# An attention and ternary feed-forward block on one core: the last chunk gets an instruction order of its own

## The chip, the core and the metric

The kernel runs on one core of a Trainium2 chip. The core has five engines with a queue each, and every queue issues its instructions in the order in which the program names them: PE multiplies matrices, DVE and POOL compute elementwise, ACT evaluates functions, SP issues the transfers. Data lie in SBUF; PE writes its results to PSUM. The metric is the device time of one execution in microseconds (us), as the median of several runs. In the profile "PEld" is the loading of PE's weights, and L12 is line 12 of the kernel before.

## What is computed

The input has 8 sequences of 1024 rows of 512 numbers. It goes through causal attention with 16 heads of 32, with a score that falls by one per position, then through a feed-forward layer with quantized activations and ternary weights, each with a layernorm ahead of it, a layernorm behind it and a residual sum:

```python
scores = jnp.einsum('bhid,bhjd->bhij', Q, K) / jnp.sqrt(jnp.float32(hd))
scores = jnp.where(causal_mask, -jnp.inf, scores) + decay      # decay = -(i - j)
attn = jax.nn.softmax(scores, axis=-1)
...
xh = x @ H                                # Hadamard
xq = _quantize_activations(xh)            # 4 bits, scale = max|row| / 7
wq = _ternary_quantize_ste(weight)
return jnp.einsum('bsi,oi->bso', xq, wq)
...
x = x + _layernorm(_L0_attn_ref(_layernorm(x, axis=-1), ...), axis=-1)
x = x + _layernorm(_L0_ffn_ref(_layernorm(x, axis=-1), L0_ffn_weight), axis=-1)
```

## The kernel before, in words

The 8192 rows are cut into 16 chunks of 512 rows, a chunk into 4 tiles of 128 rows. Since the decay makes far keys negligible, a block of 128 queries looks only at its own keys and the 128 before. That this is allowed is shown by a bound on the scores, which is collected over the chunks in `allmax` and compared at the end of the chunk before the last (L832 to L834); the flag `ok` decides whether a general version runs behind the fast one.

**Attention.** A chunk has 8 units, one for each half of the chunk (256 queries) and each group of 4 heads. A unit goes through five steps. `scores` (L522) is 24 matmuls on PE and four exponentials on ACT, which write `pr`; the tile `s` in PSUM has one buffer, so the scores of a unit wait for the exponentials of the unit before. `mask` (L551, POOL) clears what lies ahead of the query. `add_keys` (L564, POOL) adds the two key blocks into `both`, which has one buffer. `values` (L574) is 24 matmuls with the values and 8 with ones over `both`, into `av`. `divide` (L602, four DVE instructions) writes the quotient into `oT`.

**Rest.** What follows for a tile is the generator `rest` (L167). Every `next` on it issues one step, up to a `yield`:

1. `xr`: the rows are loaded again (SP)
2. o: output projection, 8 matmuls
3. y: bias, statistics (DVE), then 1/sd and `ca` (POOL, L119, L120, L187)
4. `x1`, `u`, `w`: residual sum and the first two Hadamard stages, five DVE instructions (L190 to L199), each with two inputs in SBUF
5. wT: 4 transposes, copy (ACT)
6. h: 8 matmuls, Square with a sum on ACT (L219, its output `sq` is not used), 1/sd `rb` on POOL (L221, L222)
7. maximum `sc` of h (DVE, L229), its scaling by `rb` and the reciprocal `isc` (L230 to L233)
8. `qf` (ACT, L236), `qi` (DVE, L238)
9. qiT: 4 transposes, copy (ACT)
10. f: 4 matmuls
11. `y2` (DVE, L250)
12. statistics of `y2` (DVE), 1/sd and `cc` (POOL)
13. layernorm (ACT, L258), residual sum (POOL, L259), output (SP, L260)

**The order by hand.** Inside `manual_schedule` the order of calls is the order in every queue. In the loop over chunks (L736) each round handles two units (a "pair of slots") of a chunk, and between their steps it issues steps of two tiles, `rest_a` (the newer) and `rest_b` (the older, the `rest_a` of the round before), the projections of the next chunk (`proj`) and the norms of the one after. `next(rests_due)` hands out the next tile and lets the one after it issue its `xr`. A tile runs some six units behind the attention. `bank(...)` names which of three PSUM banks (`held`, `one`, `two`) the next product takes. The last chunk goes through the same loop with `proj` empty; its tiles 2 and 3 and the remaining steps of tile 1 follow in the tail (L836 to L840), in an order written as letters. Tile names here: 15.2 is tile 2 of chunk 15.

The buffers that matter: `y`, `u`, `w`, `wT`, `y2` one, `xr` and `pr` two, `x1` three.

Of the kernel before, what the change touches and what calls it, by code (L numbers as in the profile page):

```python
# [24 lines left out]
NG = H // HPG  # L25
# [9 lines left out]
SLACK = 1.01  # L35


BAND_LIMIT = 12.5
NORM, REST = 4, 13
@with_exitstack  # L40
def sandwich_kernel(
    ctx: ExitStack,
# [14 lines left out]
    nc = tc.nc  # L57
# [51 lines left out]
    allmax = const.tile([P, 1], F32, name="allmax")  # L109
# [57 lines left out]
    def rest(pools, n, row0, oT):  # L167
# [8 lines left out]
        row, small = pools.row, pools.small  # L176
# [15 lines left out]
        half = D // 2  # L192
        u = row.tile([P, D], F32, tag="u", name=f"u_{n}", bufs=1)
# [11 lines left out]
        wT = row.tile([P, KD, P], F32, tag="wT", name=f"wT_{n}", bufs=1)  # L205
        nc.scalar.copy(wT, pt)  # L206
        yield
        xh = pools.ps_m.tile([P, D], F32, tag="pm", name=f"h_{n}_ps")
        for k in range(KD):
# [4 lines left out]
                start=True,  # L214
                stop=True,
            )
        sq = row.tile([P, D], BF16, tag="xh2", name=f"xh2_{n}", bufs=1)
        var = small.tile([P, 1], F32, tag="var", name=f"var_{n}")
        nc.scalar.activation(sq, xh, AF.Square, accum_out=var)  # L219
        rb = small.tile([P, 1], F32, tag="rstd1", name=f"rstd_b_{n}")  # L220
        nc.gpsimd.tensor_scalar(rb, var, 1.0 / D, EPS, ALU.mult, ALU.add)  # L221
        nc.gpsimd.tensor_tensor(rb, rb, neghalf[:, :1], ALU.pow)  # L222
# [4 lines left out]

        sc = small.tile([P, 1], F32, tag="sc", name=f"sc_{n}")
        nc.vector.tensor_reduce(sc, xh, AX.X, ALU.max, apply_absolute_value=True)  # L229
        nc.vector.tensor_scalar(sc, sc, rb, SCALE_MIN, ALU.mult, ALU.max)  # L230
        isc = small.tile([P, 1], F32, tag="isc", name=f"isc_{n}")
        nc.vector.reciprocal(isc, sc)
# [13 lines left out]
        yield  # L246
        acc = project(pools, f"f_{n}", lambda k: qiT[:, k, :], lambda k: ternT[:, k, :])
        yield
        y2 = row.tile([P, D], F32, tag="y2", name=f"y2_{n}", bufs=1)
        nc.vector.scalar_tensor_tensor(y2, acc, sc, wscale_row, ALU.mult, ALU.mult)  # L250
        yield
        mvc = stats(small, y2, f"c_{n}")
# [25 lines left out]
    def band():  # L278
# [4 lines left out]
        big = es.enter_context(tc.tile_pool(name="big", bufs=2))  # L283
# [4 lines left out]
        small, row = pools.small, pools.row  # L288
# [199 lines left out]
        def diagonal(col, n):  # L488
            diag = row.tile([P, P], F32, tag="diag", name=f"diag_{n}", bufs=1)
            nc.vector.tensor_scalar(diag, ident, col, None, ALU.mult)  # L490
            return diag

        def spread_max(diag, n):

            ps = pools.ps_m.tile([P, P], F32, tag="pm", name=f"m_ps_{n}")
            nc.tensor.matmul(ps, ones, diag, start=True, stop=True)
            m = small.tile([P, 1], F32, tag="spread", name=f"spread_{n}")
            nc.vector.tensor_reduce(m, ps, AX.X, ALU.max)
            return m

        class Unit:
# [59 lines left out]
                    channel_multiplier=-1,  # L561
                )

            def add_keys(self):  # L564

                self.both = big.tile([P, HPG, 2, P], F32, tag="both", name=f"both_{self.n}", bufs=1)
                pr, r0 = self.pr, 1 if self.first else 0
                nc.gpsimd.tensor_tensor(  # L568
                    self.both[:, :, r0:], pr[:, :, r0:, 0, :], pr[:, :, r0:, 1, :], ALU.add
                )  # L570
                if self.first:
                    nc.gpsimd.tensor_copy(self.both[:, :, 0], pr[:, :, 0, 1, :])
# [44 lines left out]
        chunks = [Chunk(at) for at in range(B * NCHUNK)]  # L617
# [22 lines left out]
        ch = chunks[0]  # L640
# [6 lines left out]
        r = rstd_of(small, mv[:, :, 1], TPC, "rstd_x0")  # L647
# [13 lines left out]
        for i in range(3 * KD):  # L661
# [4 lines left out]
            which, o = divmod(i, KD)  # L666
# [32 lines left out]
        def steps(gen, count):  # L699
            for _ in range(count):  # L700
                if gen is not None:
                    next(gen)

        def products(proj, count):
            for _ in range(count):
                if proj:
                    proj.product()

        def drains(proj, count):
            for _ in range(count):  # L710
                if proj:
                    proj.drain()

        def ahead(gens):

            held = None
# [16 lines left out]
        held, one, two = 0, 1, 2  # L733
        unit = None
        rest_a = rest_b = None
        for at, ch in enumerate(chunks):  # L736
            before = chunks[at - 1] if ch.c else None
            nxt = chunks[at + 1] if at + 1 < len(chunks) else None
            proj = Projections(nxt, ch if nxt.c else None) if nxt else None
            ch.oT = [  # L740
                big.tile([P, NG, 2 * P], F32, tag="oT", name=f"oT_{ch.n}_{half}")
                for half in range(2)
            ]
            for u in range(0, 2 * NG, 2):

                new = Unit(ch, before, u)
                new.scores()
                if proj and u == 0:
                    proj.combine(0)
                if unit:  # L750
                    unit.values()
                    unit.divide()
                unit = new
                steps(rest_a, 1)
                if proj and u >= 4:
                    proj.square()
                unit.mask()
                unit.add_keys()
                bank(one)
                products(proj, 1)  # L760
                drains(proj, 1)
                norm = next(norms_due)
                steps(norm, 1)
                bank(two)
                products(proj, 1)
                drains(proj, 1)
                rest_b = rest_a
                bank(held)
                steps(rest_b, 1)
                steps(norm, 1)  # L770
                rest_a = next(rests_due) if at or u >= 4 else None
                bank(one)
                steps(rest_a, 1)
                bank(two)
                steps(rest_b, 1)
                steps(rest_a, 1)
                if proj and u == 0:
                    proj.combine(1)
                if proj and u >= 4:
# [11 lines left out]
                products(proj, 1)  # L791
                steps(rest_b, 1)
                if proj and u >= 4:
                    proj.largest()
                new.mask()
                steps(rest_a, 1)
                drains(proj, 1)
# [7 lines left out]
                products(proj, 1)  # L805
                drains(proj, 1)
                if u == 6:
                    bank(held)
                    steps(rest_a, 1)
                    bank(one)  # L810
                    products(proj, 1)
                    bank(two)
                    if proj:
                        proj.shift()
                    drains(proj, 1)
                    bank(held)
                    products(proj, 1)
                    drains(proj, 1)
                    bank(two)
                    held, two = two, held  # L820
                else:
                    bank(one)
                    steps(rest_a, 1)
                    bank(held)
                    products(proj, 1)
                    drains(proj, 1)
                    bank(one)
                    held, one, two = one, two, held
                steps(rest_a, 1)
                steps(rest_b, 1)  # L830
                steps(rest_a, 1)
            if at == len(chunks) - 2:  # L832
                okm = spread_max(diagonal(allmax, "all"), "all")
                nc.vector.tensor_scalar(ok, okm, (BAND_LIMIT / SLACK) ** 2, None, ALU.is_le)  # L834

        unit.values()  # L836
        unit.divide()
        tails = {"r": rest_a, "a": next(rests_due), "b": next(rests_due)}
        for which in "rrarbarrabraabaabbababaabbabbb":
            next(tails[which])  # L840
        es.close()


# [215 lines left out]
    ok = const.tile([P, 1], I32, name="ok")  # L1059
    with tc.manual_schedule():  # L1060
        band()
# [47 lines left out]
```

## Time and profile before

| what | us |
|---|---|
| median of 3 runs (lowest to highest) | 1482.47 (1480.69 to 1483.7) |
| the profiled execution | 1484.03 |
| its span, first to last instruction | 1482.3 |
| PE, DVE, POOL, ACT busy in it | 1385.1, 1020.1, 916.0, 686.7 |
| mean granted clock of PE | 0.981 |
| scores of the last chunk's first unit begin | 1354.11 |
| values of its last unit begin | 1430.97 |
| last instruction on POOL ends | 1478.12 |

The span is what the profile covers; the 1.7 us around it belong to the execution but to no instruction. Busy time of PE is the time in which matmuls were under way, which says little about how well they are used; the granted clock says what share of its full clock PE was given. In a timeline a line gives start and duration, engine, line, operation, output and inputs with their shapes, the count, and in brackets how long the engine had been idle and whom it waited for. In the chain of waits each line is a piece of the path that ended last.

### The profile page before, as it was taken

What the parts mean: (1) busy time and instruction counts of PE and PEld (TensorE: products, weight loads), DVE (VectorE), ACT (ScalarE), POOL (GpSimd) and SP (SyncE); (2) the same over time, 40 slices, a digit from 0 to 9 for tenths busy, and PEclk for the clock granted to TensorE, in tenths of its full rate; (3) what the DMA queues carried; (4) which work ended last, traced back from release to release, by engine and by line L of the source; (5) the groups of instructions that cost most, each with busy time, mean ns of one, the idle gap of its engine ahead of it and who ended that gap; (6) DMA issues with size and microseconds to landing.
All of it is one profiled execution on the core that took longest, in us unless ns stands there. A gap on an engine that the chain in (4) does not pass through costs nothing.

```text
span 1482.3 us, 29278 instructions
## 1 busy us (share of the span) xinstructions
PE 1385.1 (93%) x11508; PEld 970.8 (65%) x11508; DVE 1020.1 (69%) x2159; ACT 686.7 (46%) x1176; POOL 916.0 (62%) x1284
## 2 busy tenths in 40 slices
PE   5999999999999999999999999999999999997763
PEld 2476777767767776677767677666767777674431
DVE  1557767677777767777777777777777777675553
ACT  2344454545545454454545455454545545352431
POOL 2365757566575766667575666658666675663653
PEclk9999999999999999999999999999999999998995
DMA  4210110111011101101111111011101101000000
GB/s 152 70 31 14 44 44 31 35 44 44 23 44 44 43 24 44 44 29 37 44 43 32 35 44 35 31 44 44 34 32 44 44 23 37 29 30 15 29 29 23
DMA packets 31777, 57.87 MB, mean 39 GB/s; under 512 B 4240, under 2 KB 4368, under 8 KB 31632
## 3 DMA queue, kind: packets, MB, share of 16 engines
q1 hardware_dynamic: 30768, 54.87, 11.3%
q8 instruction: 93, 1.52, 0.5%
q10 hardware_dynamic: 864, 1.05, 0.2%
q14 instruction: 52, 0.43, 0.1%
HBM read 39.13 MB, written 16.78 MB: 38 GB/s over the span
## 4 chain that ended last, share of the span: by engine, by line
PE 72%; DVE 21%; POOL 3%; issue 2%; ACT 1%; DMA 1%; SPq 0%; POOLq 0%; ACTq 0%; DVEq 0%
PE o_ps L153 15%; PE k_ps L388 13%; PE q_ps L388 9%; PE v_ps L388 7%; PE s L530 7%; PE av L583 6%; PE h_ps L210 4%; PE av L592 3%; DVE u L195 2%; DVE w L198 2%; DVE w L199 2%; PE f_ps L153 2%; DVE x L190 2%; DVE st_a L126 2%; DVE y L183 2%
## 5 line engine op out<-in xcount | busy, mean ns | idle before, releaser
L543 ACT ACTIVATE pr<-s,bias 128x512 f32<-128x512 f32 (+1 forms) x512 | 295.9, 661 | 171.0 <-PE s L530 154.6
L568 POOL TENSOR_TENSOR both<-pr 128x1024 f32<-128x1024 f32 (+1 forms) x128 | 269.5, 2105 | 5.6
L153 PE MATMUL o_ps<-wo_sb,oT 128*128 128x512 f32 x512 | 239.8, 612 | 0.0
L554 POOL TENSOR_SCALAR_AFFINE_SELECT pr<-pr 128x1024 f32<-128x1024 f32 x128 | 152.4, 1191 | 124.3 <-ACT pr L543 124.1
L183 DVE TENSOR_TENSOR y<-o_ps,bo 128x512 f32<-128x512 f32 x64 | 44.3, 691 | 172.1 <-PE o_ps L153 172.1
L153 PEld LDWEIGHTS o_ps<-wo_sb,oT 128*128 128x128 f32 x512 | 94.7, 195 | 96.3 <-issue 95.4
L530 PE MATMUL s<-qT,kT 32*128 32x128 f32 (+1 forms) x2816 | 143.0, 330 | 0.0
L530 PEld LDWEIGHTS s<-qT,kT 32*128 32x128 f32 x2816 | 115.4, 187 | 32.9 <-issue 22.5
L583 PE MATMUL av<-pr,v 128*32 128x128 f32 (+1 forms) x2816 | 132.3, 318 | 0.0
L119 POOL TENSOR_SCALAR rstd_a<-mv_a 128x1 f32<-128x1 f32 x64 | 14.3, 224 | 181.4 <-DVE mv_a L127 181.4
L219 ACT ACTIVATE xh<-h_ps 128x512 bf16<-128x512 f32 x64 | 38.3, 598 | 155.7 <-PE h_ps L210 155.7
L141 ACT ACTIVATE xn<-xc,nmr,rstd_n 128x512 f32<-128x512 f32 x60 | 48.8, 813 | 127.0 <-POOL nmr L139 127.0
L583 PEld LDWEIGHTS av<-pr,v 128*32 128x32 f32 x2816 | 75.2, 110 | 38.2 <-issue 1.4
L229 DVE TENSOR_REDUCE sc<-h_ps 128x1 f32<-128x512 f32 x64 | 44.1, 690 | 69.8 <-ACT xh L219 69.8
L206 ACT COPY wT<-wT_ps 128x512 f32<-128x512 f32 x64 | 37.5, 586 | 116.7 <-PE wT_ps L204 116.7
L259 POOL TENSOR_TENSOR y<-y,x 128x512 f32<-128x512 f32 x64 | 81.7, 1276 | 1.9 <-ACT y L258 1.9
L592 PE MATMUL av<-both,ones 128*32 128x256 f32 x1024 | 79.3, 381 | 2.1 <-POOL both L568 2.1
L119 POOL TENSOR_SCALAR rstd_c<-mv_c 128x1 f32<-128x1 f32 x64 | 14.8, 231 | 98.4 <-DVE mv_c L127 97.6
L210 PE MATMUL h_ps<-had_sb,wT 128*128 128x128 f32 x512 | 69.0, 278 | 5.8 <-ACT wT L206 5.8
L210 PEld LDWEIGHTS h_ps<-had_sb,wT 128*128 128x128 f32 x512 | 67.5, 194 | 10.4 <-ACT wT L206 7.4
L153 PE MATMUL f_ps<-ternT,qiT 128*128 128x512 bf16 x256 | 67.4, 387 | 1.6 <-ACT qiT L245 1.6
L608 DVE STREAM_TRANSPOSE sumT<-av 128x256 f32<-128x256 f32 x128 | 55.4, 433 | 14.2 <-PE av L592 14.2
(194 smaller groups left out, 3051.1 us busy)
## 6 DMA issues: line engine op xcount, KB each, us to landing
xr<-in_x SPq DMA_DIRECT2D x64, 256.0 KB, 3.0
out<-y SPq DMA_DIRECT2D x64, 256.0 KB, 2.0
xc<-in_x SPq DMA_DIRECT2D x60, 256.0 KB, 2.9
wk_sb<-in_wkT ACTq DMA_DIRECT2D x4, 256.0 KB, 5.5
x<-in_x SPq DMA_DIRECT2D x4, 256.0 KB, 5.0
wq_sb<-in_wqT SPq DMA_DIRECT2D x4, 256.0 KB, 4.7
wf_sb<-in_wf SPq DMA_DIRECT2D x4, 256.0 KB, 5.4
wv_sb<-in_wvT SPq DMA_DIRECT2D x4, 256.0 KB, 5.2
```

What stands on the lines that cost most here:

```text
L153: nc.tensor.matmul(ps, lhs(k), rhs(k), start=(k == 0), stop=(k == KD - 1))
L183: nc.vector.tensor_tensor(y, ps, bo2, ALU.add)
L210: nc.tensor.matmul(xh[:, k * P : (k + 1) * P], wT[:, k, :], had_sb if k else had0_sb, start=True, stop=True,)
L259: nc.gpsimd.tensor_tensor(y2, y2, x1, ALU.add)
L388: nc.tensor.matmul(ps[:, o, :], a[:, i, osl], b[:, i, :], start=(i == 0), stop=(i == HB - 1))
L530: nc.tensor.matmul(s[:, hh, sc : sc + w], kc.kT[hsl, g, at * P : (at + 1) * P], ch.qT[hsl, g, q0 + qc : q0 + qc + w], start=True, stop=True,)
L543: nc.scalar.activation(pr[:, :, r0:, own, cols], s5[:, :, r0:, own, cols], AF.Exp, bias=ch.bias[:, own, h : h + 1],)
L554: nc.gpsimd.affine_select(out=own, in_=own, compare_op=ALU.is_ge, fill=0.0, base=0, pattern=[[0, HPG], [0, 2], [1, P]], channel_multiplier=-1,
L568: nc.gpsimd.tensor_tensor(self.both[:, :, r0:], pr[:, :, r0:, 0, :], pr[:, :, r0:, 1, :], ALU.add)
L583: nc.tensor.matmul(av[hh * HD : (hh + 1) * HD, 0, qc : qc + w], kc.v[:, at, h * HD : (h + 1) * HD], pr[:, hh, sc : sc + w], start=(at_part ...
L592: nc.tensor.matmul(av[hh * HD : (hh + 1) * HD, 1, :], ones[:, :HD], self.both[:, hh].rearrange("p r c -> p (r c)"), start=True, stop=True, ...
L608: nc.vector.transpose(st.rearrange("p b c -> p (b c)"), av[:, 1, :])
```

## The change

- `rest` gets a fourteenth step: the maximum and its scaling are two steps. In the first 15 chunks they are called one right after the other.
- The Square writes its unused output into `wT` instead of a tile of its own, and `y2` has two buffers.
- `add_keys` can be given an engine.
- The loop runs over the first 15 chunks. The last chunk has its own sequence: one pair of units ahead, then a loop over three pairs, then a tail. In it a tile does only o and y in the pair in which it is handed out; x1 to y2 follow in the next pair and the last two steps in the one after (`late`). The first unit's key sum of each of the three pairs is on DVE.
- The bound's diagonal is issued at the end of the pair u = 2, its matmul and comparison at the end of u = 4 of the last chunk.
- The tail handles three tiles and the late one, in an order that names the banks too.

```diff
-NORM, REST = 4, 13
+NORM, REST = 4, 14
...
-        sq = row.tile([P, D], BF16, tag="xh2", name=f"xh2_{n}", bufs=1)
         var = small.tile([P, 1], F32, tag="var", name=f"var_{n}")
-        nc.scalar.activation(sq, xh, AF.Square, accum_out=var)
+        nc.scalar.activation(
+            wT.rearrange("p k c -> p (k c)"), xh, AF.Square, accum_out=var
+        )
...
         nc.vector.tensor_reduce(sc, xh, AX.X, ALU.max, apply_absolute_value=True)
+        yield
         nc.vector.tensor_scalar(sc, sc, rb, SCALE_MIN, ALU.mult, ALU.max)
...
-        y2 = row.tile([P, D], F32, tag="y2", name=f"y2_{n}", bufs=1)
+        y2 = row.tile([P, D], F32, tag="y2", name=f"y2_{n}", bufs=2)
...
-            def add_keys(self):
+            def add_keys(self, engine=nc.gpsimd):
...
-                nc.gpsimd.tensor_tensor(
+                engine.tensor_tensor(
...
-        for at, ch in enumerate(chunks):
+        for at, ch in enumerate(chunks[:-1]):
...
                 steps(rest_a, 1)
                 steps(rest_b, 1)
-                steps(rest_a, 1)
-            if at == len(chunks) - 2:
-                okm = spread_max(diagonal(allmax, "all"), "all")
-                nc.vector.tensor_scalar(ok, okm, (BAND_LIMIT / SLACK) ** 2, None, ALU.is_le)
-
+                steps(rest_a, 2)
+
+
+        ch, before = chunks[-1], chunks[-2]
...
+        new = Unit(ch, before, 0)
+        new.scores()
         unit.values()
         unit.divide()
-        tails = {"r": rest_a, "a": next(rests_due), "b": next(rests_due)}
-        for which in "rrarbarrabraabaabbababaabbabbb":
-            next(tails[which])
+        unit = new
+        steps(rest_a, 1)
+        new = Unit(ch, before, 1)
+        new.scores()
+        unit.mask()
+        unit.add_keys()
+        rest_b, rest_a = rest_a, next(rests_due)
+        bank(held)
+        steps(rest_b, 1)
+        bank(one)
+        steps(rest_a, 1)
+        bank(two)
+        steps(rest_b, 1)
+        steps(rest_a, 1)
+        unit.values()
+        steps(rest_b, 1)
+        new.mask()
+        new.add_keys()
+        unit.divide()
+        unit = new
+        for u in range(2, 2 * NG, 2):
+            late, rest_b, rest_a = rest_b, rest_a, next(rests_due)
+            steps(rest_b, 1)
+            new = Unit(ch, before, u)
+            new.scores()
+            unit.values()
+            unit.divide()
+            unit = new
+            unit.mask()
+            bank(held)
+            steps(rest_b, 1)
+            bank(one)
+            steps(rest_b, 2)
+            steps(late, 1)
+            steps(rest_b, 1)
+            new = Unit(ch, before, u + 1)
+            new.scores()
+            bank(two)
+            steps(rest_a, 1)
+            unit.add_keys(nc.vector)
+            steps(rest_b, 1)
+            new.mask()
+            steps(late, 1)
+            bank(held)
+            steps(rest_b, 1)
+            unit.values()
+            steps(rest_a, 1)
+            new.add_keys()
+            unit.divide()
+            unit = new
+            bank(one)
+            steps(rest_b, 2)
+            if u == 2:
+                diag = diagonal(allmax, "all")
+            elif u == 4:
+                bank(held)
+                okm = spread_max(diag, "all")
+                nc.vector.tensor_scalar(ok, okm, (BAND_LIMIT / SLACK) ** 2, None, ALU.is_le)
+            one, two = two, one
+
+        late, rest_b, rest_a = rest_b, rest_a, next(rests_due)
+        rest_c = next(rests_due)
+        tails = {"l": late, "b": rest_b, "a": rest_a, "c": rest_c}
+        steps(rest_b, 1)
+        unit.values()
+        unit.divide()
+        order = "b0 b1 b l b a2 b l b0 a b1 c0 b a c a2 a1 a a c a b c0 c2 c c a0 a1 b c a c0 a c2 c a c c"
+        for step in order.split():
+            if step[1:]:
+                bank((held, one, two)[int(step[1:])])
+            next(tails[step[0]])
```

More of the change, by code (lines that the diff above doesn't have):

```diff
@@ L702, in steps @@
                     next(gen)
[L704 to L712, printed above, removed]
         def ahead(gens):
@@ L735, in band @@
         rest_a = rest_b = None
-        for at, ch in enumerate(chunks):
+        for at, ch in enumerate(chunks[:-1]):
             before = chunks[at - 1] if ch.c else None
-            nxt = chunks[at + 1] if at + 1 < len(chunks) else None
-            proj = Projections(nxt, ch if nxt.c else None) if nxt else None
+            nxt = chunks[at + 1]
+            proj = Projections(nxt, ch if nxt.c else None)
             ch.oT = [
@@ L747, in band @@
                 new.scores()
-                if proj and u == 0:
+                if u == 0:
                     proj.combine(0)
@@ L754, in band @@
                 steps(rest_a, 1)
-                if proj and u >= 4:
+                if u >= 4:
                     proj.square()
@@ L759, in band @@
                 bank(one)
-                products(proj, 1)
-                drains(proj, 1)
+                proj.product()
+                proj.drain()
                 norm = next(norms_due)
@@ L764, in band @@
                 bank(two)
-                products(proj, 1)
-                drains(proj, 1)
+                proj.product()
+                proj.drain()
                 rest_b = rest_a
@@ L776, in band @@
                 steps(rest_a, 1)
-                if proj and u == 0:
+                if u == 0:
                     proj.combine(1)
-                if proj and u >= 4:
+                if u >= 4:
                     bank(held)
@@ L790, in band @@
                 bank(held)
-                products(proj, 1)
+                proj.product()
                 steps(rest_b, 1)
-                if proj and u >= 4:
+                if u >= 4:
                     proj.largest()
@@ L796, in band @@
                 steps(rest_a, 1)
-                drains(proj, 1)
+                proj.drain()
                 steps(rest_b, 1)
@@ L804, in band @@
                 bank(two)
-                products(proj, 1)
-                drains(proj, 1)
+                proj.product()
+                proj.drain()
                 if u == 6:
@@ L810, in band @@
                     bank(one)
-                    products(proj, 1)
+                    proj.product()
                     bank(two)
-                    if proj:
-                        proj.shift()
-                    drains(proj, 1)
+                    proj.shift()
+                    proj.drain()
                     bank(held)
-                    products(proj, 1)
-                    drains(proj, 1)
+                    proj.product()
+                    proj.drain()
                     bank(two)
@@ L824, in band @@
                     bank(held)
-                    products(proj, 1)
-                    drains(proj, 1)
+                    proj.product()
+                    proj.drain()
                     bank(one)
@@ L830, in band @@
                 steps(rest_b, 1)
-                steps(rest_a, 1)
-            if at == len(chunks) - 2:
-                okm = spread_max(diagonal(allmax, "all"), "all")
-                nc.vector.tensor_scalar(ok, okm, (BAND_LIMIT / SLACK) ** 2, None, ALU.is_le)
+                steps(rest_a, 2)
+        ch, before = chunks[-1], chunks[-2]
+        ch.oT = [
+            big.tile([P, NG, 2 * P], F32, tag="oT", name=f"oT_{ch.n}_{half}") for half in range(2)
+        ]
+        new = Unit(ch, before, 0)
```

## The prediction

> **What bounds the kernel now.** I read the table by stage first, then the chain of waits and the timeline of the last chunk. The diff leaves the order of the first 15 chunks as it is, so the question is what the last 130 us hold. Columns of the table: stretch, length, then busy time (and instructions) of PE, weight loads, DVE, ACT, POOL, granted clock, DMA share, GB/s.
>
> ```profile
> 60.00:1350.00 1290.00, 1261.30 (x10724) 906.26 (x10722) 934.58 (x1975) 623.33 (x1072) 831.90 (x1152) 1.00 0.11 36
> 1354.00:1377.00 23.00, 16.17 (x145) 9.17 (x144) 11.67 (x22) 6.69 (x11) 7.43 (x11) 0.72 0.08 24
> 1396.30:1413.60 17.30, 12.01 (x141) 6.97 (x140) 9.77 (x24) 8.07 (x14) 11.96 (x15) 1.00 0.10 31
> 1431.00:1482.30 51.30, 22.49 (x97) 10.92 (x96) 19.64 (x44) 10.13 (x18) 17.48 (x30) 0.64 0.08 27
> 1416.80:1419.60 2.80, 0.00 (x0) 0.00 (x0) 2.37 (x8) 1.48 (x3) 2.72 (x4) 1.00 0.17 66
> 1432.10:1436.90 4.80, 0.64 (x8) 0.16 (x8) 2.78 (x9) 1.18 (x2) 3.28 (x4) 0.81 0.10 37
> ```
>
> Until 1350 us PE is busy 98%: nothing there can pay. In the last chunk (no projections left) PE does 12.0 of 17.3 us per pair of slots at full clock, and 22.5 of 51 us in the tail. No engine is full; a chain of waits sets the pace. One pair of it:
>
> ```profile
> 1390.96 2.43 ACT pr L543 x4
> 1393.46 1.39 POOL pr L554
> 1394.93 0.24 POOL rstd_c L119
> 1396.45 2.32 POOL both L568
> 1398.86 0.19 POOL rstd_b L221
> 1401.91 0.35 DVE qi L238
> 1402.71 3.49 PE o_ps L153 x8
> 1407.06 1.13 PE s L530 x24
> ```
>
> The exponential, the mask, POOL's 2.3 us key sum, the Hadamard tile's rstd (queued behind that sum), quantization, o (3.49) and the next scores stand in series. Last, the timeline at the chunk's start, where DVE is blocked, and at the end:
>
> ```profile
> 1352.57 0.70 DVE L490 TENSOR_SCALAR diag_all<-ident,allmax 128x128 f32<-128x128 f32 x1
> 1353.41 0.77 PE L496 MATMUL m_ps_all<-diag_all,ones 128*128 128x128 f32 x2 [3.16 <-DVE diag_all L490]
> 1360.04 2.34 POOL L568 TENSOR_TENSOR both<-pr 128x1024 f32<-128x1024 f32 x1
> 1360.53 2.13 DVE L238 TENSOR_SCALAR qi<-qf 128x512 bf16<-128x512 f32 x1
> 1467.50 1.26 POOL L259 TENSOR_TENSOR y<-y,x 128x512 f32<-128x512 f32 x1 [0.93 <-ACT y L258]
> 1472.64 0.75 DVE L250 SCALAR_TENSOR_TENSOR y<-f_ps,sc,wscale_row 128x512 f32<-128x512 f32 x1 [7.67 <-DMA out<-y]
> ```
>
> PE waits 3.16 us for the check's diagonal. The quantization takes 2.13 instead of its usual 0.43: it ends 0.28 after the POOL instruction that was there first. I therefore let a DVE instruction that reads SBUF twice (or qi) wait for a running POOL instruction, and POOL for such a DVE one. And y2 of the last tile waits for the output transfer of the tile before.
>
> **Part by part.** Scores of 2 slots, Hadamard and so on do not change in number; I lay the new order out queue by queue with these durations.
>
> *Max and scale apart, Square into wT.* In the first 15 chunks the two steps are called back to back, so the order is the old one. Square writes 128x512 fp32 instead of bf16; the copy L206 of that form takes 0.586, Square 0.598: I take 0. Both ends: -1 to +2 us over 60 tiles, hidden by PE's 98%. It waits on h anyway, and wT has no reader left.
>
> *Bound check.* Diagonal, matmul, reduce and compare leave the head. Scores move from 1354.11 to the end of h, 1350.25: -3.9. In mid chunk the diagonal goes behind y2 on DVE (0.3, up to 0.7; behind it x1 of the next tile), the matmul behind f on PE (0.4), the reduce behind y2 (0.3 + 0.15). All but 0.3 of it lies where DVE waits for POOL's key sum; without that cover 1.2.
>
> *y2 with two buffers.* Tile b's f was ready at 1466.65, its y2 began at 1472.64: up to 5.8 us. With the new order some of it returns: 15.3 takes the buffer of 15.1.
>
> *First pair.* Scores 1350.25-1351.4, exponential 1351.7-1354.1, mask -1355.3, qi blocked to 1355.6, key sum -1358.0. Second slot's exponential ends 1357.9, ACT then copies qiT (-1358.55); o of 14.2 runs meanwhile -1359.6, f -1360.5. On POOL the second slot's mask stands behind the rstd of o: -1363.8; its key sum and the next mask take turns with x1, u, u, w, w on DVE, which end 1369.2. Transposes, copy and h take 2.5 (as at 1374.61-1377.05): h ends 1371.7.
>
> *A pair*, counted from the end of h. PE: scores to 1.1, o to 4.7. ACT: Square 0.1-0.8, exponential 1.25-3.67, qf to 4.5. DVE: max 0.83-1.5, stats of the late tile to 2.45, scale to 3.05. The key sum on DVE is not in the trace: 256 columns take 0.42, 512 0.69, so 1024 take 1.23 (against POOL's 2.36; bounds 1.1 and 3.4, the upper if it waits for a POOL key sum). It is blocked by POOL's rstd and ends at 4.5; POOL's cc waits behind it; qi, queued behind it, gets to 4.9, o's y and stats to 6.55. PE: qiT 5.35, values and sums 6.7, f 7.65. DVE: divide 8.35, y2 9.1. POOL: mask 5.05-6.2, residual sum -7.5, rstd and ca -8.75, other slot's key sum 8.8-11.15. x1, issued at 9.1, waits for that (11.75), the next mask slips in (12.9), u and w end at 14.3; plus 2.5: **16.8** a pair, against 17.3. o has left the chain; POOL's key sum before x1 has come in. With the diagonal 17.15. h of the third pair: 1371.7 + 17.15 + 16.8 = 1405.65.
>
> SP: xr of a tile two on takes the buffer that x1 has yet to read, so its DMA waits at the head of SP's queue until that x1 is done. Behind it stands only the output of the late tile, issued at 7.5 of the same pair, after x1 of that pair (which ended before h): no cost.
>
> *Tail*, from that h. Nine steps more than before (39 against 30, three of them by the split), three tiles interleaved. The last values start at 8.4. x1 of 15.1 waits to 11.15, w ends 13.2, h 15.7; o of 15.2 19.3; scale 18.75, qf 19.6, qi 20.2; y of 15.2 20.9; f of 15.1 22.4; o of 15.3 25.95; h of 15.2 28.4, its scale 30.8; DVE then x1 to w of 15.3, 33.15; h 35.65, scale 38.05, qf 38.95; qi 39.6 behind POOL's residual sum; qiT, copy, f 41.8. y2 of 15.3 waits for the output of 15.1 (39.35 + 3.75, landing as at 1468.78) and ends 43.9; stats 44.8, POOL's four small ones 46.5, ACT 47.35, POOL 48.7. From values to end 40.3, against 1430.97-1478.12 = 47.15.
>
> **The clock.** All that is at full clock: end 1405.65 + 48.7 = 1454.3, 23.8 under 1478.1. The Trainium skill, "TensorE: Matmul & The Clock Gate", section "Why this matters for your kernels", advises no PE gap over about 3 us between bursts, else the clock halves. My longest gap in a pair is 2.55 (11.8 to 14.35): by the rule all stays warm and the 23.8 stand. The row 1432.1:1436.9 says otherwise: 0.64 busy in 4.8 us, no single gap over 2.83, and the next o ran 5.92 instead of 3.65. My pair has 0.6 busy from 9.5 to 14.35, the same. Yet 1416.8:1419.6, with nothing in 2.8 us, kept 1.00. So I take two of three pairs cold: scores 2.09 and o 5.4 end 2.75 later and y with them, +5.5. Tail: wT +0.35, two h +0.9 each, two qiT +0.2 each, f +0.9: +3.5. Sum -23.8 + 9.0 = **-14.8** (all warm -23.8; three cold pairs -12.0, or -8.3 with their wT and h cold too).
>
> **Rivals.**
> - *The order pays nothing*: another wait replaces o in each pair, only check and buffer count: -3.9 - 5.8 = -9.7, 1472.8. For it: 16.8 is hardly under 17.3. Against: before's first two pairs took 22.9 and 19.3.
> - *All warm* by the rule: -23.8, 1458.7.
> - *Slower: the SBUF lock between DVE and POOL, on a cold PE.* Place: qi and the key sum on DVE behind mask and residual sum, each pair (1.11 + 1.26 = 2.4), with scores, o, wT, h cold (+4.0): pair 23.2, three times +6.4; tail +3.5 cold and +2.5 for two qi behind residual sums; first pair cold as measured (22.9 - 17.3 = 5.6) instead of 4.0, +1.6. 26.8 lost against 23.8 won: +3, 1486. It decides from a pair of about 22.5 on. For it: 2.13 and 22.9 in the trace. Against: POOL has 10.0 us of work a pair and seldom stands ahead of every DVE step.
> - *Half of that*: 1476 to 1484.
>
> **The numbers.** The profiled run took 1484.03, 1.7 around its span of 1482.3; -14.8 gives 1469.2. It was 1.6 above the median of the three runs; on the median 1482.47 it is 1467.7. Chances: as laid out, with one to three cold pairs (1465 to 1474) 0.50; order pays nothing 0.20; all warm 0.10; half lock 0.12 (half of it faster than -0.2%); slower 0.08. A measurement of this kernel tells about 0.2%, 3 us, from no change: faster 0.86, same 0.06, slower 0.08. Low end 1459 takes in the warm case, high end 1479 the half lock.
>
> **What would show it.** Right: no change before 1350; scores at 1350.3; h to h about 17 where the clock is 1.00 and 19.5 where not; key sum 1.23 on DVE; DVE's x1 idle or stretched behind POOL's key sum; about 44 us from last values to end. Wrong: pairs above 22 with full clock, x1 ahead of POOL's key sum throughout (pair under 15.5), or a first stage that moved.

## The result and the profile after

| | before | after |
|---|---|---|
| median (lowest to highest) | 1483.09 (1480.69 to 1485.58, 4 runs) | 1462.87 (1462.33 to 1463.34, 4 runs) |
| ratio, 95% interval | | 0.9863 (0.9846 to 0.9881) |
| profiled execution; its span | 1484.03; 1482.3 | 1463.16; 1461.5 |
| mean granted clock | 0.981 | 0.984 |
| scores of the last chunk begin, after the start of the h ahead of them | 4.92 | 0.99 |
| from the start of the last values to the end of POOL's last instruction | 47.15 | 40.2 |

The kernel became 20.2 us (1.4%) faster; 15 were forecast, and 1462.87 lies in the range. The table by stage of the kernel after, for its three stretches from h to h and the rest (columns as in the prediction):

```profile
1348.40:1370.50 22.10, 16.44 (x201) 9.94 (x200) 13.85 (x26) 10.27 (x18) 11.59 (x11) 0.87 0.11 37
1370.50:1389.70 19.20, 15.55 (x145) 9.31 (x144) 13.50 (x26) 8.07 (x14) 9.43 (x13) 0.77 0.10 29
1389.70:1407.10 17.40, 14.21 (x146) 8.68 (x146) 12.82 (x27) 8.07 (x14) 9.47 (x13) 0.89 0.10 32
1407.10:1457.10 50.00, 31.76 (x181) 16.48 (x180) 29.88 (x67) 16.01 (x28) 23.39 (x44) 0.77 0.08 28
```

The granted clock (third figure from the right) is under 1 in all four: this kernel too loses time to the clock, and the pair with the lower clock (0.77) is the longer one. The chain of waits of the last of these pairs, from the end of one h to the end of the next:

```profile
1389.68 2.07 PE s L532 x24
...
1392.99 1.27 ACT pr L545 x2
1394.25 0.68 ACT qf L238
1394.95 0.77 DVE qi L240
...
1396.17 1.00 PE av L585 x24
...
1399.22 0.74 DVE y L252
...
1400.27 1.20 DVE x L190
...
1402.71 1.25 DVE w L199
...
1404.65 0.59 ACT wT L206
...
1405.29 1.83 PE h_ps L210 x8
```

There is no o and no POOL instruction in it any more: the chain goes from the scores over exponential, quantization and values to `y2`, and then to x1 (`x` L190) and w of the tile whose o and y are long done. POOL shows only as a brake: `qi` takes 0.77 instead of 0.43 because the mask is ahead of it, x1 takes 1.20 instead of 0.75, the last w 1.25 instead of 0.42. The timeline of the kernel after gives the places that the prediction named:

```profile
1348.38 1.16 PE L532 MATMUL s<-qT,kT 32*128 32x256 f32 x24
...
1392.47 1.22 DVE L570 TENSOR_TENSOR both<-pr 128x1024 f32<-128x1024 f32 x1
...
1393.09 0.73 POOL L257 TENSOR_SCALAR cc<-mv_c,rstd_c 128x1 f32<-128x1 f32 x1
...
1398.54 2.37 POOL L570 TENSOR_TENSOR both<-pr 128x1024 f32<-128x1024 f32 x1
...
1400.27 1.19 DVE L190 SCALAR_TENSOR_TENSOR x<-y,rstd_a,xr 128x512 f32<-128x512 f32 x1
...
1451.24 0.75 DVE L252 SCALAR_TENSOR_TENSOR y<-f_ps,sc,wscale_row 128x512 f32<-128x512 f32 x1 [1.78 <-PE f_ps L153]
...
1455.78 1.26 POOL L261 TENSOR_TENSOR y<-y,x 128x512 f32<-128x512 f32 x1 [0.93 <-ACT y L260]
```

The scores follow h at once, with no 3.16 us of waiting for the diagonal. The key sum takes 1.22 on DVE, and POOL's `cc` behind it 0.73 instead of 0.27. x1 stands behind POOL's key sum, which ends at 1400.91. The last `y2` waits for its own product f, no longer for a transfer.

In the two profiles the end of POOL's last instruction moved by 21.1 us, from 1478.12 to 1457.04. The h of tile 15.1 cuts the last chunk into pairs and tail; these are its lines, before and after:

```profile
1429.86 1.16 PE L210 MATMUL h_ps<-had_sb,wT 128*128 128x128 f32 x8 [0.73 <-ACT wT L206]
...
1421.81 1.34 PE L210 MATMUL h_ps<-had_sb,wT 128*128 128x128 f32 x8 [0.73 <-ACT wT L206]
```

Of the 21.1 us, 1.8 lie ahead of the last chunk, 3.9 at its first scores, 2.3 between these scores and this h (75.75 us before, 73.43 after), and 13.0 between this h and the end (48.26 and 35.23). So against this execution of the kernel before, the pairs themselves became hardly shorter, and most of the gain lies in the tail, 5.6 of it by the buffer (see the first experiment).

### The profile page after: what moved, and what is told of

Read it like the earlier page. It is cut to its first block, busy times and chain, and to the rows that moved or that the text cites. A ratio compares the mean times of both kernels' runs of the same rounds, so it can differ in the third digit from the quotient of the medians.

```text
span 1461.5 us, 29036 instructions
## 1 busy us (share of the span) xinstructions
PE 1383.2 (95%) x11508; PEld 971.8 (66%) x11508; DVE 1030.6 (71%) x2162; ACT 685.7 (47%) x1176; POOL 906.1 (62%) x1281
## 3 DMA queue, kind: packets, MB, share of 16 engines
q10 hardware_dynamic: 864, 1.05, 0.2%
## 4 chain that ended last, share of the span: by engine, by line
PE 74%; DVE 21%; POOL 2%; issue 2%; ACT 1%; DMA 0%; SPq 0%; POOLq 0%; ACTq 0%; DVEq 0%
PE o_ps L153 15%; PE k_ps L390 13%; PE q_ps L390 9%; PE v_ps L390 7%; PE s L532 7%; PE av L585 6%; PE h_ps L210 4%; PE av L594 3%; DVE u L195 2%; DVE w L198 2%; PE f_ps L153 2%; DVE x L190 2%; DVE w L199 2%; DVE st_a L126 1%; DVE y L183 1%
## 5 line engine op out<-in xcount | busy, mean ns | idle before, releaser
L570 POOL TENSOR_TENSOR both<-pr 128x1024 f32<-128x1024 f32 (+1 forms) x125 | 262.5, 2100 | 5.4
L218 ACT ACTIVATE wT<-h_ps 128x512 f32<-128x512 f32 x64 | 38.2, 597 | 157.9 <-PE h_ps L210 157.9
L204 PE MATMUL wT_ps<-ident,w 128*128 128x128 f32 x256 | 44.6, 287 | 21.0 <-DVE w L199 10.7
```

The lines of the kernel that those rows point to most:

```text
L570: engine.tensor_tensor(self.both[:, :, r0:], pr[:, :, r0:, 0, :], pr[:, :, r0:, 1, :], ALU.add)
```

## The experiments

Theory: the new order carries most of the gain, because o, y and their statistics leave the chain of a pair; check and buffer add about 10. Rival: check and buffer are what counts, and the rest would be as good in the old order. A run's ratio is to the kernel before, timed in turn with it on the same chip. For the kernel before that gave 1482.38 (39 runs, 1478.0 to 1488.1), 1483.18 (11 runs) and 1483.82 (9 runs) as medians in the three groups of runs; what is said to be so much above the kernel after compares medians, which carries about 2 us of uncertainty. What a profile shows is one execution. The length of a pair is taken from h to h in the new order, and from scores to scores, which begin when h ends, in the old one.

### Parts of the change in the old order

**Square into wT and two `y2` buffers, in the kernel before.**

```diff
...
-        nc.scalar.activation(sq, xh, AF.Square, accum_out=var)
+        nc.scalar.activation(
+            wT.rearrange("p k c -> p (k c)"), xh, AF.Square, accum_out=var
+        )
...
-        y2 = row.tile([P, D], F32, tag="y2", name=f"y2_{n}", bufs=1)
+        y2 = row.tile([P, D], F32, tag="y2", name=f"y2_{n}", bufs=2)
```

> The kernel before with the Square's output in wT and two buffers for y2, nothing else. Theory (the gain is a sum of three parts: check, buffer, order): the last tile's y2 no longer waits for the output of the tile before, it starts 0.1 to 0.3 us after its f; time before minus 5.8 us, 1477.3 on a before of 1483.1. Rival A (the order alone does it, the tail in the old order is held by something else next): the wait moves to another step, minus 0 to 2 us. In the first 15 chunks both expect nothing: L219 at 0.60, stage times equal within 0.5 us.

Measured: 1484.64, ratio 1.0014 (1.0003 to 1.0024). From h of tile 15.2 to the end it took 22.0 us instead of 27.6, so the buffer did bring its 5.6 there. The pairs ahead of it lost that again: the o of five tiles ran 5.26 to 6.09 (before: 5.48, 5.35, 3.65, 3.65, 5.92), and a pair took 20.1 to 24.6 us. Why o ran slowly in all five here, and in three of five before, is not shown.

**The check at mid chunk, in the kernel before.**

```diff
+                if not proj and u == 2:
+                    diag = diagonal(allmax, "all")
+                elif not proj and u == 4:
+                    bank(two)
+                    okm = spread_max(diag, "all")
...
-            if at == len(chunks) - 2:
-                okm = spread_max(diagonal(allmax, "all"), "all")
...
```

> The kernel before, with the bound's diagonal at the end of pair u = 2 and its matmul and comparison at the end of u = 4 of the last chunk, in the old order of everything else. Theory: scores of the last chunk start at the end of h, 3.9 us earlier, and the pairs keep 22.9, 19.3, 17.3, 17.3: minus 3.9 us, about 1479. Rival B (the check's gap of 3.16 us is what sent the clock down, so it also costs what the cold clock cost behind it): the first two pairs fall towards 17.3 as well, minus 3.9 and up to 7.6 more, 1471.5 to 1475.

Measured: 1486.87, ratio 1.0035 (1.0027 to 1.0044), slower. The scores did begin earlier, but then `qi` lost against POOL's key sum twice (2.23 and 2.49 us instead of 0.43).

**Both, in the kernel before.**

> The kernel before with both: two buffers for y2 and the check in mid chunk. Theory: the two add up, minus 9.7 us, 1473.4, and the new order is worth the remaining 10 us of the changed kernel. Rival B: minus 9.7 and up to 7.6 more, 1466 to 1470, and the order is worth 3 to 7 us. Rival A: minus 4 to 6, 1478.

Measured: 1478.37, ratio 0.9972 (0.9959 to 0.9986): -4.0, where the parts as I had priced them make -9.7. The timeline of this run shows one reason:

```profile
1393.94 2.34 POOL L569 TENSOR_TENSOR both<-pr 128x1024 f32<-128x1024 f32 x1
1394.32 2.25 DVE L239 TENSOR_SCALAR qi<-qf 128x512 bf16<-128x512 f32 x1
...
1397.02 6.26 PE L153 MATMUL o_ps<-wo_sb,oT 128*128 128x512 f32 x8
```

In the old order `qi` comes up within 0.6 us of the moment at which POOL's key sum starts. Here POOL is first by 0.38, and `qi` ends 0.29 after it. In the same pair of slots the check's diagonal (0.71) had stood on DVE ahead of it. PE then waits 4.09 us for `qi`, its clock halves, and the pair takes 25.0. In the kernel before, one `qi` was ahead by 0.05 and took 0.42.

With check and buffer already in, the new order gains in both parts: from the chunk's first scores to the h of 15.1 this run takes 83.5 us (73.4 in the kernel after), and from that h to the end 41.7 (35.2). So some 10 us lie in the pairs and 6 in the tail. What the order of the tail is worth alone no run tells.

### Parts of the change taken out of the new order

**The check back at the end of the chunk before the last.**

```diff
+            if at == len(chunks) - 2:
+                okm = spread_max(diagonal(allmax, "all"), "all")
...
-            if u == 2:
-                diag = diagonal(allmax, "all")
...
```

> The changed kernel with the check at the end of chunk 14 again. Theory: scores of the last chunk wait for the diagonal, plus 3.6 us (3.9 less the 0.3 that the diagonal takes in mid chunk), 1466.5. Rival B: the cold stretch follows, plus 3.6 and another 2 to 5 us in the first pair, 1468.5 to 1471.5.

Measured: 1470.32, ratio 0.9915 (0.9902 to 0.9928): 7.4 above the kernel after. The scores come 3.9 later; 4.9 more are lost in the first pair, where `qi` now meets the key sum (2.11 us, 0.52 behind it) and o runs 5.20; 1.6 come back later. By the timeline of this run:

```profile
1358.64 2.35 POOL L570 TENSOR_TENSOR both<-pr 128x1024 f32<-128x1024 f32 x1
1359.16 2.11 DVE L240 TENSOR_SCALAR qi<-qf 128x512 bf16<-128x512 f32 x1
...
1361.70 5.20 PE L153 MATMUL o_ps<-wo_sb,oT 128*128 128x512 f32 x8
```

**One `y2` buffer.**

```diff
-        y2 = row.tile([P, D], F32, tag="y2", name=f"y2_{n}", bufs=2)
+        y2 = row.tile([P, D], F32, tag="y2", name=f"y2_{n}", bufs=1)
```

> The changed kernel with one y2 buffer. The y2 of the last tile then waits until the output of the tile before has landed, as in the kernel before (there 5.8 us): its f ends at 1451.15, the output of 15.2 would be issued near 1450.5 and take some 2 to 3.7, so +2 to +5, 1465 to 1468. Rival: in the new tail the two last tiles lie far enough apart that the buffer is worth under 1 us.

Measured: 1472.26, ratio 0.9927 (0.9914 to 0.9941): 9.4 above the kernel after, more than either expected. The timeline of this run:

```profile
1432.20 0.75 DVE L252 SCALAR_TENSOR_TENSOR y<-f_ps,sc,wscale_row 128x512 f32<-128x512 f32 x1 [2.79 <-DMA out<-y]
...
1452.48 0.75 DVE L252 SCALAR_TENSOR_TENSOR y<-f_ps,sc,wscale_row 128x512 f32<-128x512 f32 x1 [1.82 <-DMA out<-y]
...
1460.11 0.75 DVE L252 SCALAR_TENSOR_TENSOR y<-f_ps,sc,wscale_row 128x512 f32<-128x512 f32 x1 [5.94 <-DMA out<-y]
```

Three tiles wait, not one: 15.1 for the output of 15.0, 15.2 for that of 15.1, and 15.3 for that of 15.2. For the last, the two f lie too close together: from the `y2` of 15.2 to its landed output it takes 7.6 us. The other two wait because the last steps of a tile stand late in the new order: the `y2` of 15.1 begins at 1432.20, but its output is issued only at 1450.34.

**o and y at the head of the tile's own pair, instead of in the pair ahead.**

```diff
             late, rest_b, rest_a = rest_b, rest_a, next(rests_due)
-            steps(rest_b, 1)
+            bank(two)
+            steps(rest_b, 3)
...
-            bank(two)
-            steps(rest_a, 1)
             unit.add_keys(nc.vector)
...
             unit.values()
-            steps(rest_a, 1)
             new.add_keys()
```

The pair ahead of the loop loses its o and y in the same way, and the tail begins with `bank(two)` and three steps of `rest_b`.

> The changed kernel, but o and y of a tile are issued at the head of the tile's own pair, ahead of its x1, instead of a pair earlier. If the early o is what pays, o (3.65 at full clock, 4.9 at half) is back on the chain of three pairs: +10 to +15, to 1473 to 1478. Rival: o is hidden behind other work anyway and the order of the small steps pays: under +4, 1463 to 1467.

Measured: 1489.47, ratio 1.0041 (1.0027 to 1.0054): 26.6 above the kernel after and slower than the kernel before. The pairs take 25.5, 24.8 and 23.8 where the kernel after has 19.2, 17.7 and 16.5; the tail is nearly the same (35.7 and 35.2 from the last of these h). In the first third of the pair that starts at 1397.1, everything up to `qi` lies at the same distance from h as in the kernel after. Then comes, by the timeline of this run:

```profile
1411.00 3.70 PE L153 MATMUL o_ps<-wo_sb,oT 128*128 128x512 f32 x8 [1.07 <-DVE y L252]
...
1414.74 0.69 DVE L183 TENSOR_TENSOR y<-o_ps,bo 128x512 f32<-128x512 f32 x1 [3.41 <-PE o_ps L153]
...
1416.77 0.57 POOL L120 TENSOR_TENSOR rstd_a<-rstd_a,neghalf 128x1 f32<-128x1 f32 x1
1417.37 0.75 DVE L190 SCALAR_TENSOR_TENSOR x<-y,rstd_a,xr 128x512 f32<-128x512 f32 x1 [0.99 <-POOL rstd_a L120]
```

o waits until `y2` has read the same PSUM bank, then o takes 3.70, and y, its statistics and 1/sd 2.6 more before x1 can start at 20.27 after h (12.67 in the kernel after). The values ahead of f ran at half clock besides (f 1.5 later). My +10 to +15 had counted o alone. So what the early pair takes off this chain is not the 3.65 of o but some 6 us of o, y, statistics and 1/sd: x1 starts 7.16 after `y2` starts, instead of 1.05. This is the price of this one place for o, behind `y2`, in its bank and ahead of the next scores. In the old order o stands in the tile's own pair too, and pairs of 17.3 occur (the chain in the prediction has no y or statistics in it); a better place for o in its own pair was not tried in the new order.

**All key sums on POOL; both slots' key sums on DVE.**

```diff
-            unit.add_keys(nc.vector)
+            unit.add_keys()
```

> The changed kernel with all key sums on POOL, as before. My sum: the first slot's key sum takes 2.36 instead of 1.23 and stands on POOL behind the late tile's cc and ahead of the second mask; DVE is free 1.2 us earlier for qi, which however then waits for POOL; values wait, divide ends about 1.5 later: plus 1.5 to 2 us a pair, plus 4 to 6 us, 1467 to 1469. Rival (POOL has room, 10 of 17 us a pair, and PE hides it): plus 0 to 1.5 us.

```diff
-            new.add_keys()
+            new.add_keys(nc.vector)
```

> The changed kernel with the second slot's key sum on DVE too, so POOL has none in the three pairs. My sum: x1 no longer waits for POOL's 2.36 us at the end of a pair, but 1.23 us stand ahead of divide on DVE: minus 0.5 to 1 us a pair, minus 1.5 to 3 us in all, 1460 to 1461.5. Rival (DVE becomes the bound, its 11.7 us of a pair become 12.9 and lie on the chain): plus 1 to 3 us.

Measured: all on POOL 1466.92, ratio 0.9887 (0.9872 to 0.9903), 4.05 above the kernel after; both on DVE 1463.27, ratio 0.9864 (0.9849 to 0.9879), no difference. With all on POOL, `qi` takes 1.26 to 1.50 in the three pairs. With both on DVE the x1 is rid of POOL's key sum but DVE has 1.22 more to do ahead of it.

### The clock

**Idle matmuls in the pairs.** Seven bf16 matmuls that nobody reads, ahead of wT in the three pairs of the kernel after.

```diff
+        def fill(at, count):
...
+            banks.named = at
+            warm = banks.tile([P, D], F32, tag="pm", name=f"warm_{next(fills)}")
...
+            for _ in range(count):
+                nc.tensor.matmul(warm, ident_bf, ternT[:, 0, :], start=True, stop=True)
...
             unit.mask()
+            fill(held, 7)
             bank(held)
```

> The changed kernel with 7 idle matmuls of 128x512 in bf16 (1.6 us) in each of the three pairs, ahead of the Hadamard transposes. Clock theory: Hadamard and scores run at 1.16 instead of 2.08, o at 3.65, a pair takes 16.8 as worked out at full clock instead of 19.2 and 17.4, minus 3 to 6 us, 1457 to 1460. Rival (the new order hides the cold clock, its pairs are bound by DVE and POOL): less than 1.5 us of gain, or up to 1 us lost because the transposes wait for the idle matmuls.

Measured: 1459.89, ratio 0.9838 (0.9824 to 0.9851). All h, scores and o of the pairs run at full clock (1.16, 1.16, 3.70), and h follows h by 16.3 and 16.2.

**The same, and in the tail** 4 ahead of wT of 15.2 and 14 ahead of wT of 15.3.

```diff
+        for at, step in enumerate(order.split()):
+            if at == 0:
+                fill(held, 4)
+            elif at == 22:
+                fill(held, 14)
```

> The changed kernel with 7 idle bf16 matmuls ahead of wT in the three pairs (1459.9) and, in the tail, 4 more ahead of wT of 15.2 and 14 ahead of wT of 15.3; nobody reads their results. If the tail's half clock still costs (h 2.08 instead of 1.16 twice, f 1.89 instead of 1.04 twice, wT 1.24 instead of 0.60, o of 15.2 5.03 instead of 3.65), 1.5 to 3 come off: 1457 to 1458.5. Rival: the tail is bound by DVE's and POOL's steps and the fillers only delay: 1459.5 or more.

Measured: 1457.25, ratio 0.9826 (0.9813 to 0.9839), the fastest of all, 5.6 under the kernel after. The table by stage of this run for two pairs:

```profile
1379.00:1396.00 17.00, 14.53 (x169) 8.30 (x161) 14.11 (x28) 8.19 (x14) 10.25 (x15) 1.00 0.13 42
1396.00:1413.00 17.00, 13.91 (x151) 7.29 (x147) 14.07 (x29) 8.19 (x14) 10.35 (x14) 1.00 0.09 32
```

**Idle matmuls in the old order**: 10 and 4 at two places of a pair and 10 at the head of the tail, on top of check and buffer.

```diff
                 rest_b = rest_a
+                if not proj:
+                    fill(one, 10)
                 bank(held)
...
+                if not proj:
+                    fill(held if u == 6 else one, 4)
...
         unit.divide()
+        fill((pools.ps_m.turn + 1) % 3, 10)
```

> The old order with two y2 buffers and the check in mid chunk (as the run with both), and with idle matmuls on PE in the last chunk: 10 of 128x512 in bf16 (about 2.2 us) ahead of each quantized tile's transposes, 4 ahead of each Hadamard transposes, 10 at the start of the tail; nobody reads them. Clock theory (the missing gain of the two parts was eaten because the clock halves in the gaps of the old order): the granted clock stays 1.00 through the four pairs, each takes 17.3 us instead of 19 to 24, and the time falls from 1478 to 1462 to 1466: the old order at full clock is as fast as the new one. Rival (the pairs are longer for another reason, the order itself): the clock rises but the pairs keep 19 us or more, and the time stays at 1475 or above; the idle matmuls may then cost 1 to 3 us.

Measured: 1473.91, ratio 0.9928 (0.9914 to 0.9943), 4.5 under the same kernel without them. Its first pairs take 17.6 and 18.1; then `qi` loses to POOL's key sum (started 0.38 and 0.16 before it; 2.24 and 2.47 us), and the pairs take 23.7 and 22. The third pair by the timeline of this run:

```profile
1389.47 2.34 POOL L569 TENSOR_TENSOR both<-pr 128x1024 f32<-128x1024 f32 x1
1389.85 2.24 DVE L239 TENSOR_SCALAR qi<-qf 128x512 bf16<-128x512 f32 x1
...
1392.55 6.39 PE L153 MATMUL o_ps<-wo_sb,oT 128*128 128x512 f32 x8
```

Neither expectation holds: the first pairs came down to near the 17.3 of full clock, but behind a lost `qi` PE waits 3.02 us for it in spite of the idle matmuls, and o runs at half clock again.

### Is the lost race the cause in the old order?

By then I held that the race between `qi` and POOL's key sum is what eats check and buffer there. This run takes the race away: in the old order with both, the even slot's key sum of the last chunk goes to DVE.

```diff
                 unit.mask()
-                unit.add_keys()
+                unit.add_keys(nc.gpsimd if proj else nc.vector)
```

> The old order with check at mid chunk and two y2 buffers (1478.4), and in the last chunk the even slot's key sum on DVE, so that no POOL key sum stands where the quantization qi goes. Theory of the race for SBUF: it was the lost race that made pairs of 20 and 25 us there; qi then takes 0.42 to 0.8 in every pair, a pair 17 to 18.5 (o stays on the chain), and the time falls by 8 to 13, to 1465 to 1470. Rival, the clock alone makes the long pairs: PE's gap between f and o stays, the clock still halves, the time stays within 3 us of 1478. In neither does it reach the changed kernel's 1462.9 unless the rstd of h, which no longer stands behind POOL's key sum, brings another 1 us a pair.

Measured: 1477.78, ratio 0.9957 (0.9943 to 0.997): no different from 1478.37. `qi` now takes 0.42 (0.76 behind the mask in the first pair), and yet the pairs take 20.2 to 20.7, as the rival expected. The theory that the race alone does it has fallen. The timeline of one of these pairs shows what holds it:

```profile
1375.95 0.42 DVE L239 TENSOR_SCALAR qi<-qf 128x512 bf16<-128x512 f32 x1
...
1376.42 0.40 PE L244 MATMUL qiT_ps<-ident_bf,qi 128*128 128x128 bf16 x4 [2.10 <-DVE qi L239]
1376.66 5.35 PE L153 MATMUL o_ps<-wo_sb,oT 128*128 128x512 f32 x8
...
1386.58 1.11 POOL L555 TENSOR_SCALAR_AFFINE_SELECT pr<-pr 128x1024 f32<-128x1024 f32 x1 [1.01 <-ACT pr L544]
1386.61 1.36 DVE L199 TENSOR_TENSOR w<-u 128x256 f32<-128x256 f32 x1
```

o runs 5.35 instead of 3.65 (+1.7), and the last w loses another race, against the mask, by 0.03 us (1.36 instead of 0.42, +0.9). Together 2.6; without them the pair of 20.2 would be 17.6. The table by stage of the next pair shows what goes ahead of a slow o:

```profile
1394.00:1397.40 3.40, 1.13 (x19) 0.60 (x10) 3.26 (x9) 1.60 (x4) 1.97 (x2) 1.00 0.47 148
1397.40:1400.80 3.40, 3.40 (x5) 1.33 (x4) 0.54 (x1) 0.49 (x1) 0.00 (x0) 0.50 0.04 11
1400.80:1404.20 3.40, 3.40 (x32) 1.71 (x30) 1.65 (x4) 0.00 (x0) 0.00 (x0) 1.00 0.00 0
```

A stretch of 3.4 us with PE at 1.13 is followed by one at half clock, and o lies in it. So in the old order there are two costs: the lost race of `qi`, which the idle matmuls left and behind which o ran at half clock as well, and the half clock on o without a lost `qi`, which this run left. Here it makes 1.7 of the 2.6 us. Taking away both at once was not tried; that this would give pairs near 17.5 is worked out, not shown.

## Where the prediction was right and where not

The sum was -14.8. In the profiles the end of POOL's last instruction moved by -21.1: 1.8 of the difference was there before the last chunk. Of this, 1.14 lies ahead of the first h of all, where it varies from run to run (120.40 us in the kernel before, 119.42 in the run with only the check moved, 119.26 in the kernel after). The other 0.66 goes with the Square's new output: from the first h to the last ahead of chunk 15 the two kernels with the old output take 1228.79 us, the twelve with the new one 1228.13 to 1228.38. Of the rest, 2.2 came in the pairs and 2.3 in the tail. All of these lie on the same side.

- **Nothing before 1350 us, Square at 0**: right but for these 0.4 to 0.7 us. The Square took 0.597 against 0.598.
- **Scores at the head, -3.9**: right, -3.93.
- **Check under cover**: right. Reduce and compare (0.43) lie between `y2` and x1, while POOL's key sum holds x1 anyway; the diagonal ran 1.47, itself behind a key sum. That the check's place also decides whether `qi` of the first pair meets the key sum I had not seen: out of the head it is worth 7.4, not 3.9.
- **Key sum on DVE 1.23**: right, 1.22. POOL's `cc` waits behind it, 0.73.
- **First pair**: its h was laid out to end at 1371.7, or 1369.9 with the 1.8; it ended at 1370.53, at half clock.
- **A pair of 16.8 to 17.15 at full clock, 19.5 with a cold o**: the mechanism held, and so did the wait of x1 behind POOL's key sum. The pairs took 19.2 and 17.4. The three o took 4.87, 3.83 and 3.70, not 5.4 twice: the half clock fell mostly on wT, h and scores, so it is partly luck that 19.2 lies so near 19.5. With idle matmuls, at full clock throughout, h follows h by 16.3 and 16.2: some 1 us less than the 17.3 of the old order at full clock.
- **The clock, +9.0**: the sign was right, the size was the term that was off. Pairs and tail came out 4.5 shorter than laid out, and taking the half clock away, as far as idle matmuls could, gave 5.6. The Trainium skill's rule ("TensorE: Matmul & The Clock Gate", "Why this matters for your kernels": no gap over about 3 us) would have left no loss in the pairs; the trace has two h of the pairs at 2.08 although no gap ahead of them is over 2.27. The row decided rightly. In the tail the rule and the trace agree: PE idles 4.35 us ahead of wT of 15.3, and the h behind it takes 2.08.
- **Tail from h of the third pair, 48.7 warm and 52.2 cold**: 49.9. I had `y2` of 15.3 wait for the output of 15.1 (1.2 us on the path); it waited only for f.
- **Rival "the order pays nothing", -9.7**: fell, and not only because the order pays. Check and buffer alone do not bring 9.7 but 4.0: I had added two prices that can't be added in the old order, because an earlier start moves `qi` and o against POOL's key sum and against the clock.
- **Rival "all warm", 1458.7**: not what the change alone gave, but with the idle matmuls the kernel takes 1457.25.
- **Rival "slower", by the SBUF lock**: `qi` does stand behind the mask in each pair, at a price of 0.33, not 2.4. From that side nothing near the 22.5 us per pair came up; pairs that long came only when o was put back into its own pair (25.5), and for another reason.

The parts don't add up in the new order either: taking out the check's place, the buffer and the early o costs 7.4, 9.4 and 26.6, against 20.2 for the whole. Each of them puts a wait back that moves other steps, in the first pair of the run with the check, for one, `qi` and o.

## What to carry to other kernels

Where a chain of waits and no engine sets the pace, take whole steps with all that hangs on them (here o with y, statistics and 1/sd, some 6 us a pair against the other place tried) out of the chain by doing them one round ahead; a single shortened wait can be eaten by the next race. Look in the timeline for DVE and POOL instructions that start within half a microsecond of each other: whichever comes first decides over 1 to 2 us, so a change that shifts one of them is priced with both outcomes. When PE is half idle anyway, a few matmuls that nobody reads, placed in its gaps, are a cheap try.

## What was not expected of the hardware

- **A race at the shared SBUF port.** The Trainium skill ("SBUF — State Buffer", "Who interferes with whom") calls the port that DVE and GpSimd (POOL) share an exclusive lock. The traces agree and give the price: `qi` took 0.42 when 0.05 us ahead of POOL's key sum, 2.25 when 0.38 behind; a w took 1.36 instead of 0.42 when 0.03 behind a mask.
- **The half clock comes in pieces.** The granted clock was 0.50 or 1.00, and its changes lay at multiples of 3.4 us, as in the table above (in the run with both: half from 1354.5, full from 1357.9, half from 1368.2, full from 1371.6). With the even slot's key sum on DVE in the old order, o once ran at half clock with no PE gap over 2.10 us in the 9 us ahead of it, and it ran at half clock in every pair, with pairs of 20.2 to 20.7. That is near six such pieces; whether the pair and the clock keep each other in step is not shown.
- **Spread.** The kernel before spread over 10 us in 39 runs and over 4.9 in the 4 timed with the kernel after; the kernel after spread over 1.0 in 4, and with idle matmuls in pairs and tail over 1.0 in 5. The old order has `qi` and POOL's key sum 0.01 to 0.6 us apart; that this makes the spread was only argued.
